# Attention's context product as two column groups of 64 on TensorE, each with the keys of its own two heads

## The chip, the core and the metric

The kernel runs on one core of a Trainium2 chip. The metric is the device time of one execution in microseconds (us): the median of six runs before the change is 1322.69 us, and the six lie between 1321.06 and 1329.03 us. All data are fp32.

A core has four compute engines with queues of their own, each of which works its instructions in order: TensorE (PE in the profile; its weight loads are listed apart as PEld), VectorE (DVE), ScalarE (ACT) and GpSimd (POOL). SyncE (SP) issues most of the DMAs. A matmul has a stationary operand, which a weight load brings into the array, and a moving operand, which streams through it. Its result goes to PSUM, where DVE and ACT read it. Each fp32 matmul of the program appears in the trace as two MATMUL records, each with a weight load; a transpose appears as one.

## The reference

The network has two layers on an input x of 16 samples, 128 channels and 32 x 32 positions. Layer 0 is a linear attention followed by a spectral filter over the tokens, layer 1 is a pair of 3 x 3 convolutions followed by routed experts. Only the attention matters here:

```python
q = jax.nn.softmax(q, axis=-2) * SCALE          # over the 1024 positions
k = jax.nn.softmax(k, axis=-1)                  # over the 32 features of a head
context = jnp.einsum('bhdc,bhec->bhde', k, v)
out = jnp.einsum('bhde,bhdc->bhec', context, q)
y = jnp.einsum('bcn,oc->bon', outf, w_out) + b_out[None, :, None]
```

There are four heads of 32 features. The kernel multiplies in another order: it forms, sample by sample, the 128 x 128 product of q and k over the 1024 positions, of which only the four 32 x 32 blocks on the diagonal (a head's queries with the same head's keys) belong to the result. It sets the rest to zero and multiplies what is left by the output weights, by the value weights and last by the normalised input.

## The kernel before

The program runs in stages: the attention with the tokens' transform (stage A, to about 395 us of the span), the spectral products (to about 685 us), the convolutions with the routing (to about 1216 us), the experts (to about 1290 us) and the output. The change touches stage A only.

Stage A is the class `Attention` (from L341) and an order written out by hand, the list `period` (L713 to L727). One pass of the loop over `p` (L731) issues one step of each kind: the name is a method of `Attention`, the number says for which sample, p + d. So seven samples are under way at once, and a period holds one `tokens`, one `context`, one `channels` and so on, each of another sample. A manual schedule (L730) keeps this order on PE, DVE, ACT and POOL as it is written. The loop starts at p = -6, so the first passes hold only the early steps, and the last passes lack them.

On PE the order in a full period is: `tokens` (8 transposes of the input, L149), `context` (L482), `channels` (8 transposes of the normalised tokens, L159), `input` (8 transposes, L154), `fold` (L495), `even` (L551), `taps_in` (L159), `odd` (L551), `q_tokens` (L149), `fold2` (L504), `k` (L436), `taps` (L618), `group` (L387), `q` (L418) and `out` (L514).

`context` multiplies, for each of the 8 blocks j of 128 positions, the queries of that block (`self.qt[:, j, :]`, stationary, 128 positions by 128 features) by the keys (`ket[:, j, :]`, moving, the same shape), and sums over j in one PSUM tile `pc` of 128 x 128. The keys come from POOL (`k_scale`, L461), the queries from ACT (`q_copy`, L474). `context_mask` (L488, DVE) multiplies `pc` by the reciprocal sums of the queries and by `mask`, which is one on the four 32 x 32 diagonal blocks and zero elsewhere, and writes `cx`. `fold` multiplies `cx` by the output weights, `fold_copy` (L499, DVE) brings the result back, `fold2` multiplies by the value weights, `fold2_copy` (L508, DVE) brings it back, and `out` applies it.

Other steps that the prediction speaks of: `moments` and `moments2` (L132, DVE, four statistics instructions on the transposes in PSUM), `tokens_copy` (L361, ACT), `q_exp` (L427, ACT), `input_copy` (L530, ACT; it follows `moments2`, which reads the same PSUM tile), `channels_copy` (L409, ACT), `out_add` (L519, DVE), `taps_add` (L625, DVE). PSUM is shared out as three large tiles, tag `big`, that go round among eleven steps of a period, and two small ones, tag `s`, which `pc` and the two `pw` take in turn.

Layer 1 holds a step of the form that the change brings in. `pool` (L1242) multiplies, for each of 8 blocks, two stationary operands of 128 x 64 by two moving operands of 128 x 128, into rows 0 to 63 and 64 to 127 of one PSUM tile `pp`:

```python
for i in range(NT):
    for jj in range(2):
        es = slice(jj * E, (jj + 1) * E)
        nc.tensor.matmul(self.pp[es, :], self.gtt[:, i, es], toks[self.b - 1 + jj][:, i, :],
```

Of the kernel before, what the change touches and what calls it, by code (L numbers as in the profile page):

```python
# [8 lines left out]
F32 = mybir.dt.float32  # L9
AF = mybir.ActivationFunctionType  # L10
ALU = mybir.AluOpType
# [3 lines left out]
P = 128  # L15
B, C, H, W = 16, 128, 32, 32
N = H * W
NT = N // 128
# [48 lines left out]
def metaformer_kernel(ctx: ExitStack, tc: tile.TileContext, io: dict, out: bass.AP):  # L67
    nc = tc.nc
# [26 lines left out]
    for n, (g_, b_, m_, v_) in enumerate(((V_G1, V_B1, V_M1, V_V1), (V_G2, V_B2, V_M2, V_V2))):  # L95
# [15 lines left out]
                name=nc.get_next_instruction_name(), ins=[], outs=[], act_func_set_id=EXP_LN  # L111
# [52 lines left out]
    with ExitStack() as l0:  # L164
# [43 lines left out]
        with ExitStack() as a0:  # L208
# [8 lines left out]
            ps = a0.enter_context(tc.tile_pool(name="aps", bufs=2, space=PSUM))  # L217
# [97 lines left out]
            mask = aconst.tile([P, P], F32, name="mask")  # L315
            nc.vector.memset(mask, 0.0)
            for h in range(HEADS):
                s = slice(h * DH, (h + 1) * DH)
# [22 lines left out]
            class Attention:  # L341
# [134 lines left out]
                def context(self):  # L476


                    self.pc = ps.tile([P, P], F32, name="pc", tag="s")
                    ket = self.ke.rearrange("p (j h) d -> p j (h d)", h=HEADS)  # L480
                    for j in range(NT):
                        nc.tensor.matmul(  # L482
                            self.pc, self.qt[:, j, :], ket[:, j, :], start=(j == 0), stop=(j == NT - 1)
                        )

                def context_mask(self):
                    self.cx = work.tile([P, P], F32, name="cx", tag="cx")
                    nc.vector.scalar_tensor_tensor(  # L488
                        self.cx, self.pc, self.qs[:, 2:3], mask, ALU.mult, ALU.mult
                    )  # L490

                def fold(self):
# [253 lines left out]
        with ExitStack() as g0:  # L746
# [61 lines left out]
            for c in range(NCH):  # L808
# [21 lines left out]
                e = cpl.tile([P, JL // RG, 2, C], F32, name="ye", tag="ye", bufs=1)  # L830
# [24 lines left out]
    with ExitStack() as c1:  # L855
# [6 lines left out]
        ps = cps.enter_context(tc.tile_pool(name="cps", bufs=2, space=PSUM))  # L862
# [559 lines left out]
        with tc.manual_schedule(engines=PINNED):  # L1422
            hs, og = {}, {}
# [29 lines left out]
        ps = c1.enter_context(tc.tile_pool(name="fps", bufs=4, space=PSUM))  # L1453
# [147 lines left out]
```

## Time and profile before

| what | value |
|---|---|
| median of six runs | 1322.69 us (1321.06 to 1329.03) |
| the profiled execution's own time | 1324.97 us |
| its span in the trace | 1323.2 us |
| PE busy in the span | 1215.8 us (92%) |
| DVE, ACT, POOL busy | 907.9, 705.1, 502.6 us |
| `context`, L482: matmul records | 256, union 31.2 us |
| mean granted TensorE clock | 0.972 |

The span is the profiled execution from its first to its last instruction; the execution's own time is 1.8 us longer. A row of the timeline holds the start in the span, the time from the first start to the last end, the engine, the line, the operation, the names, the stationary and the moving shape and the number of records; in brackets stands how long the engine was idle before it and whose end released it. A matmul's record lasts longer than its share of the engine, since matmuls are pipelined (275 ns for one of L482): what one costs is the distance from its start to the start of the next. In rows of windows the columns are: the stretch, its length, busy time and records of PE, PEld, DVE, ACT and POOL, the granted clock, the DMA share and GB/s.

### The profile page before, as it was taken

Reading aid. Unit: us, or ns where it says so; the run is one execution under the profiler, and the core shown is the slowest. Engines: PE = TensorE matmul, PEld = TensorE weight load, DVE = VectorE, ACT = ScalarE, POOL = GpSimd, SP = SyncE. Lnnn points to the kernel's source line nnn. Section 1 sums busy time; section 2 is a strip of 40 time slices with the busy share of each in tenths; the row PEclk is TensorE's granted clock in tenths of the full one; section 3 lists DMA queues with packets and bytes.
Section 4 is the critical chain, followed back from the end, with each engine's and each line's share of the span. In section 5 each row is a group of like instructions: output and inputs, shape, how many; then the busy total and the mean of one; then the engine's idle time right before and its main releaser. Section 6 shows DMA issues by size and latency. Waiting matters only on the chain. (4 is left out here: it accounts for less than half of the span.)

```text
span 1323.2 us, 33734 instructions
## 1 busy us (share of the span) xinstructions
PE 1215.8 (92%) x14116; PEld 990.3 (75%) x14116; DVE 907.9 (69%) x1982; ACT 705.1 (53%) x1424; POOL 502.6 (38%) x816
## 2 busy tenths in 40 slices
PE   4889999999998999999956999999999999996885
PEld 3677777777766888888846987989898898883443
DVE  5788788887765666677637777777777686762224
ACT  3777777777545666666623435555555454544111
POOL 2324545454585777777733121222212121110002
PEclk8999999999999999999977999999999999997997
DMA  7014343434344333333266211303122113017986
GB/s 268 17 35 142 116 139 107 146 122 127 117 146 139 129 128 127 129 125 118 98 239 179 69 47 49 93 22 109 32 80 64 33 49 127 17 33 258 374 323 254
DMA packets 87401, 162.99 MB, mean 123 GB/s; under 512 B 5584, under 2 KB 40784, under 8 KB 86864
## 3 DMA queue, kind: packets, MB, share of 16 engines
q1 hardware_dynamic: 86608, 158.33, 36.1%
q8 instruction: 111, 1.82, 0.6%
q0 software_dynamic: 640, 2.49, 0.5%
q14 instruction: 42, 0.34, 0.1%
HBM read 104.18 MB, written 56.62 MB: 122 GB/s over the span
## 5 line engine op out<-in xcount | busy, mean ns | idle before, releaser
L926 PE MATMUL pcv<-v,cw 128*128 128x256 f32 x1536 | 342.9, 380 | 0.0
L926 PEld LDWEIGHTS pcv<-v,cw 128*128 128x128 f32 x1536 | 287.2, 190 | 41.9 <-issue 5.7
L783 DVE COPY g<-pg 128x512 f32<-128x512 f32 x224 | 145.8, 686 | 90.3 <-PE pg L776 90.3
L785 ACT COPY g<-pg 128x512 f32<-128x512 f32 x288 | 153.1, 591 | 101.1 <-PE pg L776 100.9
L776 PE MATMUL pg<-ph,mst 32*128 32x128 f32 x4096 | 153.0, 284 | 4.8 <-ACT g L785 3.4
L776 PEld LDWEIGHTS pg<-ph,mst 32*128 32x128 f32 x4096 | 128.6, 187 | 30.8 <-issue 25.6
L796 PE MATMUL py<-g,v 128*32 128x128 f32 x4096 | 141.0, 278 | 7.6 <-issue 2.3
L796 PEld LDWEIGHTS py<-g,v 128*32 128x32 f32 x4096 | 106.1, 110 | 24.7 <-issue 3.9
L767 POOL TENSOR_TENSOR v<-xc 128x256 f32<-128x256 f32 x128 | 91.5, 740 | 72.1 <-PE py L796 62.8
L141 ACT ACTIVATE tok<-tok,sts 128x128 f32<-128x128 f32 x256 | 101.8, 481 | 23.5 <-POOL sts L1001 20.2
L132 DVE BATCH_NORM_STATS2 bst<-big 128x6 f32<-128x256 f32 x256 | 91.1, 416 | 19.2 <-PE big L154 12.3
L1066 POOL TENSOR_SCALAR sts<-bst 128x8 f32<-128x8 f32 x16 | 6.5, 404 | 234.9 <-DVE bst L132 234.9
L920 DVE TENSOR_TENSOR v<-pads 128x544 f32<-128x544 f32 x128 | 85.0, 723 | 9.8 <-ACT pads L1119 9.5
L618 PE MATMUL big<-u,mu 128*128 128x128 f32 (+4 forms) x384 | 86.0, 380 | 0.0
L274 POOL TENSOR_TENSOR xf<-ab 128x256 f32<-128x256 f32 x34 | 24.8, 729 | 132.8 <-DVE ab L241 132.7
L618 PEld LDWEIGHTS big<-u,mu 128*128 128x128 f32 x384 | 56.8, 191 | 18.0 <-issue 15.3
L1097 ACT ACTIVATE ct<-pcv,bn 128x256 f32<-128x256 f32 x64 | 30.2, 472 | 67.9 <-PE pcv L926 67.0
L551 PE MATMUL big<-wf,ub 128*128 128x256 f32 x256 | 62.0, 385 | 0.2
L149 PEld LDWEIGHTS big<-ident,x 128*128 128x128 f32 x384 | 46.5, 146 | 19.2 <-issue 6.9
L149 PE MATMUL big<-ident,x 128*128 128x128 f32 x384 | 52.8, 283 | 8.7 <-DVE x L1048 3.5
L1115 DVE TENSOR_TENSOR r<-pcv,cs 128x256 f32<-128x256 f32 x64 | 26.9, 420 | 48.6 <-PE pcv L926 47.8
L141 ACT ACTIVATE tt<-tt,sts 128x128 f32<-128x128 f32 x128 | 51.1, 481 | 9.8 <-POOL sts L1001 9.5
(231 smaller groups left out, 2273.1 us busy)
## 6 DMA issues: line engine op xcount, KB each, us to landing
we<-in_weight SPq DMA_DIRECT2D x32, 1024.0 KB, 10.4
vd<-xf SPq DMA_DIRECT2D x16, 1024.0 KB, 5.1
xc<-vd SPq DMA_DIRECT2D x64, 256.0 KB, 3.6
yd<-ys SPq DMA_DIRECT2D x32, 512.0 KB, 3.9
y<-yd SPq DMA_DIRECT2D x15, 896.0 KB, 6.6
x<-in_x SPq DMA_DIRECT2D x16, 512.0 KB, 4.1
mi<-in_M_phi SPq DMA_DIRECT2D x16, 512.0 KB, 4.7
xd<-x SPq DMA_DIRECT2D x16, 512.0 KB, 6.0
```

The costliest lines, as they stand in the source:

```text
L132: nc.vector.bn_stats(bst[:, j : j + 2, :].rearrange("p j s -> p (j s)"), src[:, j : j + 2, :].rearrange("p j c -> p c j"),)
L141: nc.scalar.activation(dst[:, j, :], src[:, j, :], AF.Identity, bias=nm[:, j : j + 1], scale=r[:, j : j + 1],)
L149: nc.tensor.transpose(pt[:, j, :], src[:, j * P : (j + 1) * P], ident)
L551: nc.tensor.matmul(dst, self.ub[:, q, :], wf[:, q, :], start=True, stop=True)
L618: nc.tensor.matmul(self.pa[:, a:hi], mu[:, NF - 1 - si, tap, :], self.u[:, a - tap : hi - tap], start=(tap == 0), stop=(tap == KU - 1),)
L767: nc.gpsimd.tensor_tensor(vv[:, x, 1:, bs], e, o, op)
L776: nc.tensor.matmul(pg[r][:, i], mst[rs, 4 * q + i, :], ph[rs, c, :], start=True, stop=True,)
L783: nc.vector.tensor_copy(dst, src)
L785: nc.scalar.copy(dst, src)
L796: nc.tensor.matmul(py[rows, x, kl, :], v[:, (x * NM + m) * JL + jl, 1 - ri : 3 - ri, :] .rearrange("p k b -> p (k b)"), g[:, ((x * 2 + ri) ...
L920: nc.vector.tensor_tensor(v[:, k], d[i], d[j], op)
L926: nc.tensor.matmul(pc[:, i], wt[:, dy, k, :], v[:, k, hf * HR + dy : hf * HR + dy + HR], start=(dy == 0), stop=(dy == 2),)
```

## The change

Each of the 8 matmuls of a `context` becomes two. Each takes 64 of the queries' features as stationary operand (two heads) and the 64 keys' features of the same two heads as moving operand. The first writes rows 0 to 63 of `pc`, the second rows 64 to 127, both to the same 64 columns, so `pc` is 128 x 64 instead of 128 x 128 and holds for each head its own keys and those of one neighbour. `context_mask` reads `pc` twice over, once for each half of the columns of `cx`, and multiplies by the same mask: the halves that belong to the other two heads become zero as before. Nothing else changes, and no step is moved: PE, DVE, ACT, POOL and SP have the same rows with the same waits in the same order, but for the 128 matmuls of `context` that become 256.

```diff
-                    self.pc = ps.tile([P, P], F32, name="pc", tag="s")
+                    self.pc = ps.tile([P, P // 2], F32, name="pc", tag="s")
                     ket = self.ke.rearrange("p (j h) d -> p j (h d)", h=HEADS)
                     for j in range(NT):
-                        nc.tensor.matmul(
-                            self.pc, self.qt[:, j, :], ket[:, j, :], start=(j == 0), stop=(j == NT - 1)
-                        )
+                        for g in range(2):
+                            hs = slice(g * P // 2, (g + 1) * P // 2)
+                            nc.tensor.matmul(
+                                self.pc[hs, :], self.qt[:, j, hs], ket[:, j, hs],
+                                start=(j == 0), stop=(j == NT - 1), skip_group_check=True,
+                            )
 
                 def context_mask(self):
                     self.cx = work.tile([P, P], F32, name="cx", tag="cx")
                     nc.vector.scalar_tensor_tensor(
-                        self.cx, self.pc, self.qs[:, 2:3], mask, ALU.mult, ALU.mult
+                        self.cx.rearrange("p (g e) -> p g e", g=2),
+                        self.pc.unsqueeze(1).to_broadcast([P, 2, P // 2]), self.qs[:, 2:3],
+                        mask.rearrange("p (g e) -> p g e", g=2), ALU.mult, ALU.mult,
                     )
```

## The prediction

> **What bounds the kernel now.** I read the windows first, cut at the starts of `context`, since the change lies in stage A alone. The second and third columns of a row are the length and PE's busy time:
>
> ```profile
> 54.00:66.00 12.00, 11.05 (x73) 8.53 (x72) 11.65 (x30) 10.48 (x20) 8.14 (x12) 1.00 0.00 0
> 213.40:235.30 21.90, 21.23 (x128) 16.61 (x127) 17.97 (x44) 15.92 (x34) 10.52 (x17) 1.00 0.40 120
> 342.00:357.20 15.20, 15.20 (x89) 12.14 (x88) 11.17 (x24) 9.34 (x19) 7.88 (x12) 1.00 0.47 156
> ```
>
> A full period lasts 21.89 us (`context` starts at 213.43 and 235.32) and PE is idle for 0.66 us of it. The second view is the timeline of that period, to see where PE waits and what stands close behind:
>
> ```profile
> 212.55 1.04 PE L149 MATMUL big<-ident,x 128*128 128x128 f32 x8
> 213.43 1.95 PE L482 MATMUL pc<-ke,qt 128*128 128x128 f32 x16
> 214.05 1.10 ACT L427 ACTIVATE qe<-big,qs 128x1024 f32<-128x1024 f32 x1
> 215.21 1.04 PE L159 MATMUL big<-ident,tok 128*128 128x128 f32 x8
> 215.42 0.35 DVE L488 SCALAR_TENSOR_TENSOR cx<-pc,qs,mask 128x128 f32<-128x128 f32 x1
> 215.46 1.01 ACT L361 COPY tok<-big 128x1024 f32<-128x1024 f32 x1 [0.22 <-PE pc L482]
> 216.09 1.05 PE L154 MATMUL big<-ident,x 128*128 128x128 f32 x8
> 217.18 1.42 DVE L132 BATCH_NORM_STATS2 bst<-big 128x6 f32<-128x256 f32 x4 [0.77 <-PE big L154]
> 217.20 1.89 PE L551 MATMUL big<-wf,ub 128*128 128x256 f32 x8
> 218.69 1.01 ACT L530 COPY ub<-big 128x1024 f32<-128x1024 f32 x1 [2.22 <-DVE bst L132]
> 219.76 1.09 PE L159 MATMUL big<-ident,ub 128*128 128x128 f32 x8 [0.66 <-ACT ub L530]
> ```
>
> The reader is to see that PE's one wait, at 219.76, is the end of a chain that PE itself starts: `input` (L154), `moments2` (L132), `input_copy` (L530). It begins 2.66 us after `context`, so it moves with it. **PE sets the period**, and what `context` takes less is off the period as long as nothing else becomes late. `context` takes 1.79 us (213.43 to 215.21).
>
> **How the new form runs.** The trace has its like: `pool`, with two groups of 64 stationary columns, but 128 moving columns. The third view is the timeline around one, the fourth the records' durations (minimum, median, maximum):
>
> ```profile
> 1188.38 0.60 PE L149 MATMUL big<-ident,x 128*128 128x128 f32 x4
> 1189.97 0.66 PE L149 MATMUL big<-ident,x 128*128 128x128 f32 x4 [0.99 <-DVE x L1145]
> 1190.55 1.97 PE L1242 MATMUL pp<-tt,gtt 128*64 128x128 f32 x32
> 1192.45 1.09 PE L159 MATMUL big<-ident,tt 128*128 128x128 f32 x8
> ```
>
> ```profile
> L1242 PEld LDWEIGHTS pp<-tt,gtt x256: 132/137/231, 843.7 to 1215.7; 128*64 128x64 f32 x128
> L1242 PE MATMUL pp<-tt,gtt x256: 272/273/473, 843.7 to 1215.9; 128*64 128x128 f32 x128
> ```
>
> 32 records take 1.90 us from 1190.55 to 1192.45, where 32 of L482 would take 3.57. The starts of single records show why: they come in pairs 7 ns apart, one of each group, and the pairs 0.109 us apart. So the groups run side by side.
>
> **The sum, term by term.** The distance from a matmul to the next follows the moving columns: four records of L514 (512 columns) take 1.71 us (210.84 to 212.55), 0.428 each; L551 (256) 0.215; transposes (128) 0.109. That is 0.107 for 128 and 0.002 over, hence 0.055 us for 64. Loads follow the stationary columns: when a block starts, sets of loads begin 0.028 us apart for 32 columns (L796, a set of four), 0.055 for 64 (L1242, a set of two), 0.107 for 128 (L776, a set of four). So a pair of 64-column loads, 0.055, has to fit beside a pair of 64-column streams, 0.055. That is the balance that L482 has today at 128 and 128, and there the distance is 0.1115, some 0.004 over the stream alone. I take **0.058 us a pair**; bounds are 0.055 (no such loss) and 0.109 (a pair never goes below `pool`'s).
>
> Changes of form cost something. From the last transpose to `pool`'s first pair it is 0.202 us where an ordinary distance is 0.109; the same stands at L776 to L796 and back, medians 0.200 and 0.202 of some 240. `pool`'s first pair is followed after 0.160 instead of 0.109, since its successor waits for loads that nothing covers. From the last pair to the next step it is 0.210, and that step's second transpose comes after 0.165 instead of 0.110. For the new form the first pair's follower comes after 0.110 (0.160 less the half stream) and the way out takes 0.157 (0.210 less the same).
>
> - Now: 0.109 in, 1.786 for 16 records and the way out, 0.110 to the second transpose of `channels`: 2.005 us.
> - After: 0.202 + 0.110 + 14 x 0.058 + 0.157 + 0.165 = 1.446 us.
> - Difference: **0.56 us a context**; with 0.055 it is 0.60, with everything as in `pool` (1.90 for the block, 0.09 in, 0.05 after) it is a loss of 0.26.
>
> **What of it is on the path.** In the period above these are the waits behind `context` and the distance from their release to their start today: `channels` for `out_add`, 1.17; `input` for `q_exp`'s end with its accumulator read (215.24), 0.85; `fold` for the mask (215.77), 1.21; `even` (L551) for `tokens_copy` (216.47), 0.73; `moments2` for a free DVE (216.41), 0.77. A release takes about 0.06, so the smallest leaves 0.67, and 0.56 fits. What would be late next is `even` on `tokens_copy`, 0.1 us further on; then DVE. The ring that ACT and DVE form by themselves (`input` to `input_copy` to the sums, the norms, `q_exp`, `input`) lasts the period less 0.85, about 21.05 us, so it doesn't bind at 21.33.
>
> `context_mask` keeps its 128 output columns, so I leave its 0.35 us; twice that at worst would lie in DVE's 0.77. Its PSUM operand comes earlier, but it stands behind `moments` (to 215.37) on DVE, so it starts when it did. POOL, SP and all DMAs are untouched.
>
> Not every context counts. The first (54.36) is followed by `fold` at 57.09, 0.06 after the mask on DVE, which is held by other work: nothing. Numbers 2 to 14 count in full: 13 x 0.56 = 7.3. The last two (341.93 and 357.23) have no `channels` behind them; `input` follows, on an x that `out_add` finishes 0.30 before it starts now. Of that 0.06 is the release and 0.05 the uncovered first load, so 0.2 each: 0.4. The later stages start when stage A ends and shift as a whole. **The sum is -7.7 us.** Against the profiled execution's 1324.97 us (span 1323.2) that is 1317.3; this execution is 2.3 us over the median, so I set it against the median: 1322.69 - 7.7 = 1315.0 us, 0.6% less.
>
> **A rule that speaks against it.** In L482 a load begins 3 ns after the matmul before it starts, and the distance is 0.1115 and not the 0.214 that load and stream in turn would take; in `pool` likewise a load starts 2 ns after its group's matmul. The Trainium skill, "TensorE: Matmul & The Clock Gate", section "Part 3: Packing small matmuls — row/col tiling", says that a weight load overlaps running matmuls only where their row groups differ; here both groups use all 128 rows. By that rule pairs would come 0.109 us apart and the change would lose, which is the first rival. The trace doesn't bear the rule out for these forms, so I give it little.
>
> **The rivals.**
>
> - *A pair is no faster than today's matmul* (load 0.055 and stream 0.055 in turn, or the groups one after the other): 0.109 a pair. The sum is then 0.20 to 0.26 us longer a context, over 15 contexts +3.0 to +3.9 us: 1325.7 to 1326.6, slower than before. It decides from a pair distance of 0.095 us on, where 15 distances eat the 0.56. Against it stand the loads 0.055 apart and the overlap in L482; for it, that no row has 64 moving columns. Chance 0.08.
> - *A floor between the two*: the queue must issue 64 instructions in 0.9 us, 14 ns each. The densest stretch known, L796, has four loads and four matmuls in 0.109 us, 13.6 ns each, so there is hardly reserve. A pair at 0.083 gives -2.8: 1319.9. Chance 0.11.
> - *The gain is given back*: `even` or `moments2` becomes late although 0.1 us remain by the rows, say through a slower mask on DVE. If half is lost, -3.9: 1318.8. Chance 0.05.
> - *Forecast*: pair 0.055 to 0.065, -8.4 to -6.2. Chance 0.76.
>
> **How the numbers follow.** The forecast's own range is 1314.3 to 1316.5; the median itself may lie 1 us off on either side, which gives 1313 to 1317.5. To leave out no more than 2 in 10 I reach over the floor's case to 1320; below, to 1312.5, for a smaller price of the change of form. A measurement of this kernel can tell 0.3%, 4.0 us, from no change. Faster by more takes the forecast, half of the third rival and a little of the second: 0.81. Within: the rest of these and most of the first: 0.14. Slower: 0.05.
>
> **What would show it.** In the trace after, a block of 32 records of L484 from `tokens` to `channels` should take 1.08 us instead of 1.79; the pairs should stand 0.058 apart; the distance from the last L149 to the first L484 should be 0.20; a full period should be 21.33 us with PE still idle by about 0.66 before `taps_in` and by nothing before `even`; L491, the mask, should still take 0.35; and the first L776 should start 7.7 us earlier. A distance of 0.11 between pairs, or idle time of PE before L556 of more than a tenth, would make the prediction wrong.

## The result, and the profile after

The changed kernel takes 1316.31 us in the median of 25 runs (1312.50 to 1322.92), beside 1322.96 us for the kernel before in 51 runs: a ratio of 0.9951 with a 95% interval of 0.9938 to 0.9964, or 6.5 us less (4.8 to 8.2). The forecast was 1315.0 us, 7.7 us less. The profiled execution has a span of 1315.7 us. The runs of one kernel spread with the granted clock: of the changed kernel's, those at 0.963 took 1321.7 to 1322.9 us, those at 0.972 took 1312.9 and 1315.8.

The windows first, over one full period from `context` to `context` (length, then PE's busy time and records). It is 21.32 us long where it was 21.89, and PE's idle time in it is the same but for 0.01, 0.68:

```profile
207.71:229.03 21.32, 20.64 (x143) 15.80 (x143) 17.84 (x44) 15.91 (x34) 10.53 (x17) 1.00 0.37 124
```

The timeline of that period, around `context` (L484 now; L154 is `input`, L132 `moments2`, the last row `taps_in`):

```profile
206.74 1.04 PE L149 MATMUL big<-ident,x 128*128 128x128 f32 x8
207.71 1.15 PE L484 MATMUL pc<-ke,qt 128*64 128x64 f32 x32
208.79 1.09 PE L159 MATMUL big<-ident,tok 128*128 128x128 f32 x8
209.47 0.33 DVE L491 SCALAR_TENSOR_TENSOR cx<-pc,qs,mask 128x128 f32<-128x128 f32 x1
209.72 1.04 PE L154 MATMUL big<-ident,x 128*128 128x128 f32 x8
210.79 1.42 DVE L132 BATCH_NORM_STATS2 bst<-big 128x6 f32<-128x256 f32 x4 [0.34 <-PE big L154]
213.37 1.09 PE L159 MATMUL big<-ident,ub 128*128 128x128 f32 x8 [0.66 <-ACT ub L535]
```

The reader is to see three things. From L484 to L159 it is 1.08 us where it was 1.79. The way from L149's start to L484's is 0.97 where it was 0.88: the change of form. And PE's one wait is still 0.66, since its chain moved along, while DVE's idle time before `moments2` fell from 0.77 to 0.34. The mask (L491) takes 0.33 us.

The durations of the records (minimum, median, maximum) show the narrower form:

```profile
L484 PEld LDWEIGHTS pc<-ke,qt x512: 132/138/139, 53.0 to 348.9; 128*64 128x64 f32 x171
L484 PE MATMUL pc<-ke,qt x512: 221/222/271, 53.0 to 348.9; 128*64 128x64 f32 x171
```

By the starts of single records the two groups of a pair stand 6 to 7 ns apart and the pairs 0.0583 us apart.

Two sections of time help to compare traces: the period, and stage A from the first `context` to the first L776 (in after, L781). The latter is 340.83 us before and 332.76 us after, 8.07 less. Behind it and ahead of it the two profiles differ by 0.6 us the other way on balance, in parts of the program that the change doesn't touch. Stage A still holds the distance from the first `context` to the second, which depends on how the kernel started: it lies between 10.67 and 11.95 us in the thirteen traces, and in the changed kernel itself at 11.29 and 11.95. Counted from the second `context` on, stage A is 328.89 us before and 321.47 us after, 7.42 less.

### The profile page after: what moved, and what is told of

It reads as the page before. It is cut to its first block, busy times and chain, and to the rows that moved or that the text cites. A ratio compares the mean times of both kernels' runs of the same rounds, so it can differ in the third digit from the quotient of the medians.

```text
span 1315.7 us, 34246 instructions
## 1 busy us (share of the span) xinstructions
PE 1206.9 (92%) x14372; PEld 977.6 (74%) x14372; DVE 905.1 (69%) x1982; ACT 705.1 (54%) x1424; POOL 502.4 (38%) x816
## 5 line engine op out<-in xcount | busy, mean ns | idle before, releaser
L781 PE MATMUL pg<-ph,mst 32*128 32x128 f32 x4096 | 152.8, 284 | 5.6 <-ACT g L790 4.0
L781 PEld LDWEIGHTS pg<-ph,mst 32*128 32x128 f32 x4096 | 128.5, 187 | 31.7 <-issue 25.2
L132 DVE BATCH_NORM_STATS2 bst<-big 128x6 f32<-128x256 f32 x256 | 91.1, 417 | 15.4 <-PE big L154 8.7
L556 PE MATMUL big<-wf,ub 128*128 128x256 f32 x256 | 62.0, 385 | 0.2
L149 PEld LDWEIGHTS big<-ident,x 128*128 128x128 f32 x384 | 46.6, 146 | 17.8 <-issue 7.2
L149 PE MATMUL big<-ident,x 128*128 128x128 f32 x384 | 52.8, 283 | 7.1 <-ACT tok L141 3.1
```

Source lines behind the costliest of these rows:

```text
L132: nc.vector.bn_stats(bst[:, j : j + 2, :].rearrange("p j s -> p (j s)"), src[:, j : j + 2, :].rearrange("p j c -> p c j"),)
L149: nc.tensor.transpose(pt[:, j, :], src[:, j * P : (j + 1) * P], ident)
L556: nc.tensor.matmul(dst, self.ub[:, q, :], wf[:, q, :], start=True, stop=True)
L781: nc.tensor.matmul(pg[r][:, i], mst[rs, 4 * q + i, :], ph[rs, c, :], start=True, stop=True,)
```

## The experiments

The theory: PE's loop sets the period, pairs of groups run side by side, and a pair's distance follows the moving columns. The rivals: one of the two halves of the change does it alone; the gain comes from elsewhere; the next limit is another than the forecast said.

| run | block of `context`, us | period, us | stage A, us | from the second context, us | median, us | ratio to before (95%) |
|---|---|---|---|---|---|---|
| before | 1.787 | 21.89 | 340.83 | 328.89 | 1322.96 | |
| after | 1.082 | 21.33 | 332.76 | 321.47 | 1316.31 | 0.9951 (0.9938 to 0.9964) |
| e1, after again | 1.083 | 21.33 | 333.49 | 321.54 | 1313.69 | 0.9929 (0.9898 to 0.9960) |
| e2, groups, all keys | 1.898 | 22.15 | 344.25 | 332.98 | 1326.72 | 1.0027 (1.0002 to 1.0051) |
| e3, one group after the other | 1.831 | 22.08 | 343.24 | 331.98 | 1324.85 | 1.0012 (0.9987 to 1.0037) |
| e4, four groups | 0.694 | 21.21 | 330.96 | 319.03 | 1310.50 | 0.9904 (0.9867 to 0.9941) |
| e5, two groups, half the blocks | 0.665 | 21.24 | 330.45 | 319.18 | 1308.22, one run | |
| e6, e4 with `fold` twice | 0.693 | 21.24 | 330.34 | 319.64 | 1318.02 | 0.9954 (0.9925 to 0.9982) |
| e7, after with `fold` twice | 1.082 | 21.33 | 333.23 | 321.97 | 1318.26 | 0.9958 (0.9926 to 0.9990) |
| e8, after with the mask twice | 1.082 | 21.33 | 334.34 | 322.84 | 1320.05, one run | |
| e9, e4 with `q_exp` first | 0.824 | 21.07 | 328.79 | 317.88 | 1311.83 | 0.9928 (0.9903 to 0.9953) |
| e10, e9 with `moments2` first | 0.824 | 21.07 | 329.13 | 318.46 | 1313.86 | 0.9927 (0.9899 to 0.9955) |
| e11, e4 again | 0.694 | 21.21 | 330.96 | 319.03 | 1311.74 | 0.9923 (0.9899 to 0.9948) |

Block and period are read from the full periods of each trace. Each ratio is to runs of the kernel before made beside the run (medians 1322.2 to 1322.7 us), so it isn't quite the quotient of two medians of the table. e5 and e8 have one run each, so only their traces count.

**e1: the changed kernel again.**

> The changed kernel once more, for a narrower interval and as the neighbour of the others. Theory (PE sets the period, each context is 0.56 us shorter): ratio to the kernel before 0.994 to 0.995, block of L484 1.08 us, period 21.33 us. Rival (the 6.7 us are partly the start of the kernel, whose first context began 1.3 us earlier in the profile of after): ratio 0.996 to 0.998 while the period is the same 21.33.

Period and block are the same to 0.01 us, and the ratio is 0.9929; the rival's 0.996 is the end of the interval. Of the 8.07 us in the profile of after, 0.65 were the start, since the first two contexts stand 11.29 us apart there and 11.95 in e1; counted from the second context the two traces save 7.42 and 7.35. The gain isn't an accident of one start.

**e2: the grouping without the halved stream.** `pc` is 128 x 128 again, with the old mask:

```diff
-                                self.pc[hs, :], self.qt[:, j, hs], ket[:, j, hs],
+                                self.pc[hs, :], self.qt[:, j, hs], ket[:, j, :],
```

> Two column groups of 64, but each with all 128 moving columns, and the mask as before: the grouping without the halved stream. Theory (pair distance follows the stream): pairs 0.109 us apart as in pool, block 1.90 us, 0.09 more on the way in and 0.05 behind, period 22.15 us, about 3.9 us slower than the kernel before. Rival (two groups side by side are what brings the gain, the halved keys are not needed): block near 1.1 us, as fast as after.

```profile
213.15 1.97 PE L484 MATMUL pc<-ke,qt 128*64 128x128 f32 x32
215.05 1.09 PE L159 MATMUL big<-ident,tok 128*128 128x128 f32 x8
```

The block takes 1.90 us, as `pool`'s does, and the pairs are 0.109 apart. The kernel is slower than before: +4.1 us from the second context on (+3.4 in the whole of stage A, whose first distance was short in this start, 11.28 us), ratio 1.0027. Two groups alone only cost the change of form; the gain is in the halved keys.

**e3: the halved stream without neighbours.**

```diff
-                    for j in range(NT):
-                        for g in range(2):
+                    for g in range(2):
+                        for j in range(NT):
```

> The changed kernel with the two loops exchanged: the 8 blocks of the first group, then the 8 of the second, the same 16 program matmuls with 64 moving columns. Theory (the groups must run side by side): single matmuls 0.058 us apart, 32 of them, block about 1.97 us, period about 22.25 us, some 5 us slower than before. Rival (the halved stream alone brings the gain, since neighbours overlap anyway): block near 1.1 us, as fast as after.

```profile
212.86 1.90 PE L484 MATMUL pc<-ke,qt 128*64 128x64 f32 x32
214.69 1.09 PE L159 MATMUL big<-ident,tok 128*128 128x128 f32 x8
```

Single records are 0.0583 us apart, so one alone costs what a pair costs. The gain is gone: +3.1 us from the second context on, and the ratio's interval holds 1. The block is 0.14 shorter than I expected: around the change from the first group to the second the starts come in three pairs 3 to 6 ns apart, as if the last records of one group ran beside the first of the other. So both parts of the change are needed, the halved keys and the two groups in turn.

**e4: four groups of 32.** `pc` is 128 x 32 and needs no other head's keys at all:

```diff
-                        for g in range(2):
-                            hs = slice(g * P // 2, (g + 1) * P // 2)
+                        for g in range(HEADS):
+                            hs = slice(g * DH, (g + 1) * DH)
```

> Four column groups of 32, each with its own head's 32 keys; pc is 128 x 32 and read four times over by the mask. Theory 1 (distance is the stream plus 0.004, no other floor): sets of four 0.031 us apart, block about 0.64 us, context 1.0 us shorter than in the kernel before; of that only 0.67 us a period can count, because then even waits for tokens_copy: period 21.22 us, 1.4 us faster than after, PE idle 0.3 us before even. Theory 2 (instructions cannot be issued closer than the 13.6 ns each of the densest stretch known): sets of four 0.109 us apart, block about 1.85 us, period about 22.05 us, some 2 to 3 us slower than the kernel before.

```profile
206.51 0.76 PE L484 MATMUL pc<-ke,qt 128*32 128x32 f32 x64
207.21 1.09 PE L159 MATMUL big<-ident,tok 128*128 128x128 f32 x8
208.04 0.19 ACT L427 ACTIVATION_READ_ACCUMULATOR qe<-big,qs 128x1 f32 x1
208.29 1.16 PE L154 MATMUL big<-ident,x 128*128 128x128 f32 x8
208.45 1.01 ACT L361 COPY tok<-big 128x1024 f32<-128x1024 f32 x1 [0.22 <-DVE bst L132]
209.52 1.99 PE L556 MATMUL big<-wf,ub 128*128 128x256 f32 x8
212.06 1.09 PE L159 MATMUL big<-ident,ub 128*128 128x128 f32 x8 [0.55 <-ACT ub L535]
```

Sets of four are 0.032 us apart at first and 0.036 on average in the second half, so 128 instructions go out in 0.69 us, some 5 ns each: there is no floor at 14 ns. With 0.20 in and 0.165 behind, the context is 0.94 us shorter than before, but the period only 0.68, to 21.21. That is the number that I had expected, for the reason that `even` waits for `tokens_copy`. The rows show a second wait: `input` (L154) starts 0.06 after `q_exp`'s accumulator read ends (208.23) and has 1.16 us of records instead of 1.04. The 0.3 us of idle time before `even` (L556) that I had expected aren't there, since `input` is late already; but `even` does start 0.06 after `tokens_copy` ends (209.46), and has 1.99 us of records instead of 1.89. Which of the two sets the period is what e5 to e7 and e9 ask.

**e5: half the blocks.** Only every second block of positions is summed, so half of the sum is left out:

```diff
-                    for j in range(NT):
+                    for j in range(0, NT, 2):
```

> The changed kernel (two groups) with only every second of the 8 blocks: half of the sum over the positions is left out. Block of L484 about 0.61 us, so PE alone would need a period of 20.86 us. Theory (below a saving of about 0.7 us a period something else than PE's work sets it, as with the four groups): period 21.2 us as there, with PE waiting before input for q_exp. Rival (the four groups lost 0.26 us a period to their own irregular issue): period 20.9 us.

With two groups and a context that would allow 20.86, the period is 21.24. The block takes 0.665 us, 0.05 more than expected, for which the list of waits names no cause. The limit isn't peculiar to four groups. Over eight periods PE waits in `input` for ACT as the expectation says (us in total, times, longest); the changed kernel has no such wait:

```profile
PEld big L154 <- ACT qe L427: 2.5, 8, 0.3
```

**e6 and e7: `fold` twice**, in the kernel with four groups and in the changed one:

```diff
-                    nc.tensor.matmul(self.pw, self.cx, wout, start=True, stop=True)
+                    for _ in range(2):
+                        nc.tensor.matmul(self.pw, self.cx, wout, start=True, stop=True)
```

> Four groups, and fold's matmul issued twice (0.22 us more of PE between input and even). Theory A (with four groups the ring of ACT and DVE sets the period through q_exp and input, and PE's wait before taps_in covers what lies between input and taps_in): period stays 21.21 us, PE's idle time before taps_in falls from 0.55 to about 0.35. Theory B, the step of the prediction (even is late, on tokens_copy, and sets the period): even starts 0.2 us later than with the four groups alone, period 21.35 to 21.42 us, 2 us slower than the four groups.

> The changed kernel, and fold's matmul issued twice (0.22 us more of PE between input and taps_in). Theory A (PE's loop runs over tokens, context, channels, input and then over DVE and ACT to taps_in; what PE does between input and taps_in is covered by the 0.66 us of idle time): period stays 21.33 us, idle before taps_in 0.44. Theory B (every PE instruction of a period counts, as the prediction put it: PE sets the period): period 21.55 us, 2.9 us slower than after.

The timeline of e6, then that of e7; the first row is `fold`, the second `even`, the third `taps_in`:

```profile
210.51 0.61 PE L501 MATMUL pw<-wout,cx 128*128 128x128 f32 x4
210.96 1.89 PE L557 MATMUL big<-wf,ub 128*128 128x256 f32 x8
213.29 0.87 PE L159 MATMUL big<-ident,ub 128*128 128x128 f32 x6 [0.44 <-ACT ub L536]
```

```profile
210.52 0.61 PE L501 MATMUL pw<-wout,cx 128*128 128x128 f32 x4
210.97 1.89 PE L557 MATMUL big<-wf,ub 128*128 128x256 f32 x8
213.31 0.88 PE L159 MATMUL big<-ident,ub 128*128 128x128 f32 x6 [0.44 <-ACT ub L536]
```

In both `even` starts 0.2 us later and the wait before `taps_in` is shorter, 0.44 instead of 0.55 and 0.66. The periods are 21.24, 0.03 over e4's, and 21.33: they don't follow. Work between `input` and `taps_in` is free up to that wait, and a late `even` is too. Theory B falls for both. In e6 the wait fell by less than the 0.2 us expected, since `even` starts too late there to be held by `tokens_copy`, and its records take 1.89 us again. From the second context on, stage A is 0.4 to 0.6 us longer than in e1 and e4; 0.15 to 0.18 of that lies behind each of the last two contexts. The medians of these two lie 2 to 8 us above those of their neighbours, with intervals that overlap. In the profiled executions that difference lies behind stage A, in stages that these edits don't touch: 933.6 us in e6 beside 925.6 in e4, and 931.3 in e7 beside 924.9 in e1. In e6 the clock is granted at half for 73.9 us of that time, in e4 for 58.4; by my estimate the 15.5 us between them are worth 7.8, if PE is busy in all of them. In e7 and e1 it is 59.4 and 56.7 us, which doesn't account for the 6.4; that stays open.

**e8: the mask twice on DVE**, with `for _ in range(2):` before the operation of `context_mask`.

> The changed kernel with context_mask issued twice on DVE, 0.37 us more between moments and moments2. DVE is idle for 0.34 us before moments2 in after, so moments2 starts about 0.03 us late and, lying on the loop, lengthens the period by as much: 21.36 to 21.38 us. Rival (the mask has a follower that waits, fold on PE): fold starts late, but that is covered before taps_in, so nothing more than the 0.03; if the mask were on the path the period would be 21.7 us.

The period stays 21.33 us, without the 0.03 to 0.05 expected. The two operations take 0.72 us, and `moments2` starts 3.09 us behind the start of `context`, as in after: the idle time before it took up the second mask, as the prediction had it. The longer stage A doesn't come from the periods: from the second context to the third it is 16.71 us beside 15.40 in after, and there the clock is granted at half for 6.8 us instead of 3.4.

**e9 and e10: lift the limit.** In the list `period`, over the kernel with four groups, first `q_exp` and `k_exp` change places, then also `moments2` and `group_scale` (the edit of e10, its two lines drawn into one):

```diff
-("group_root", 4), ("k_exp", 3), ("fold", 2), ("group_scale", 4), ("moments2", 1), ("q_exp", 3),
+("group_root", 4), ("q_exp", 3), ("fold", 2), ("moments2", 1), ("group_scale", 4), ("k_exp", 3),
```

> Four groups, and on ACT q_exp issued before k_exp instead of after it. Theory A (with four groups input waits for q_exp): the wait goes, input comes 0.26 us earlier, of which DVE's 0.22 us of idle time before moments2 lets nearly all pass: period 20.95 to 21.0 us, 3 us faster than the four groups alone (about 1307). Theory B (even on tokens_copy sets the period with four groups): tokens_copy stays where it is behind moments, period unchanged at 21.21.

> As the run before, and on DVE moments2 issued before the four small operations of group_scale instead of behind them, so that DVE is free 0.7 us earlier for moments2. Theory A: nothing holds input and moments2 back, PE's loop alone is left: period 20.95 us, 3.1 us faster than the four groups. If group_scale now comes late for channels_copy, the wait stands before channels_copy and odd, and the period is 21.1 or more.

The period falls to 21.07, half of the way to 20.95: theory B, in which nothing moves, is out, and `q_exp` was the limit. The size was off because the wait moved. In e9's waits of eight periods `input` no longer appears, and `channels` waits instead, which leaves its block at 0.82:

```profile
PEld big L159 <- ACT qe L427: 1.4, 8, 0.2
```

The missing part is that wait: the block is 0.13 longer than in e4. e10 changes nothing more, where 20.95 was expected: DVE is idle for 0.7 us before `moments2` and the period is the same, so DVE doesn't hold it.

**e11: four groups again.**

> The four groups again beside these two, for a fair comparison: period 21.21 us, ratio to the kernel before about 0.993 by the trace's stage A (9.9 us), between that and 0.990 as first measured.

Period 21.21, stage A 330.96 as in e4, ratio 0.9923. Counted from the second context on, four groups are 2.4 to 2.5 us shorter than the changed kernel, and they are faster than both kernels by their medians; against the changed kernel the intervals of the ratios overlap. The swap of e9 takes another 1.2 us off behind the second context (the rest of the 2.2 in stage A is the start), which the medians can't tell.

## Why the prediction was right

- **PE's loop sets the period: right, with a correction.** 0.56 us off `context` takes 0.56 off a full period (21.89 to 21.33), and e2's 0.26 more puts 0.26 on. But not all of PE counts. e7 shows that the loop runs from `input` over DVE and ACT to `taps_in`, and that PE's own work on that stretch lies beside it.
- **The price of a pair: right.** 0.058 taken, 0.0583 measured. The loads run beside the streams: a group's next load starts 2 to 3 ns after its matmul. The first rival, by which load and stream take turns, would have given 0.109. The rule of the Trainium skill behind it ("TensorE: Matmul & The Clock Gate", section "Part 3: Packing small matmuls — row/col tiling": a weight load overlaps running matmuls only where row groups differ) doesn't hold here: both groups use all rows, and the measured distance decides.
- **The change of form: right.** 0.202 in, 0.100 + 0.007 to the second pair, 0.159 out and 0.166 to the second transpose were forecast as 0.202, 0.110, 0.157 and 0.165.
- **The floor of issue: the rival is out**; e4 issues at some 5 ns an instruction.
- **Which contexts count: right but for the second and the last two.** The second gives 0.38, not 0.56 (15.78 to 15.40 to the third). Behind it PE waits 2.88 us for `fold_copy` in both kernels, and the clock is then granted at half for 3.41 us. In before (the first two rows; 0.50 is the granted clock) PE still waited in the first 0.35 of that, in e1 (the last row) it was busy in all of it:

```profile
73.64:73.99 0.35, 0.00 (x0) 0.00 (x0) 0.35 (x4) 0.32 (x3) 0.00 (x0) 0.50 0.00 0
73.99:77.05 3.06, 3.06 (x14) 3.06 (x15) 2.79 (x14) 3.03 (x9) 0.00 (x0) 0.50 0.00 0
72.80:76.21 3.41, 3.41 (x18) 3.41 (x18) 3.13 (x16) 3.38 (x9) 0.27 (x1) 0.50 0.00 0
```

  So from `fold2` to `group` it is 3.74 us in e1 and 3.56 before. The 0.18 between them, half of the 0.35, is what is missing: where the stretch fell, and not what `context` takes. e2, where PE was busy in all of it too, is 0.43 over before here, 0.17 more than the 0.26 of its period. The next twelve give 0.56 each. The last two give 0.28 together, not 0.4 (15.30 to 15.18, and 37.96 to 37.80 from the last to the first L776). There `input` waits for `out_add`, as foreseen:

```profile
332.82 1.15 PE L484 MATMUL pc<-ke,qt 128*64 128x64 f32 x32
334.27 1.16 PE L154 MATMUL big<-ident,x 128*128 128x128 f32 x8 [0.30 <-DVE x L524]
```

  The loads of L154 are 0.19 long, those of L159 0.14, and its second matmul after a wait comes after 0.21 and not 0.165. The prediction had carried over the wrong row.
- **The first context counts for nothing: right.** To the second it is 11.94 us before and 11.95 in e1, where `fold` waits for the mask:

```profile
56.19 0.49 PE L500 MATMUL pw<-wout,cx 128*128 128x128 f32 x2 [0.46 <-DVE cx L491]
```

  In the profile of after it is 11.29, but also 11.28 in e2, whose context is the longest. That distance depends on how the start of the kernel went, not on the context: after, e2, e3, e5 and e7 (11.26 to 11.29) have 3.4 us at half the clock between 48 and 52 us, just ahead of the first context, and before, e1, e4 and e11 (11.93 to 11.95) have none there. How the one leads to the other no run shows.
- **What would be late next: wrong.** The step said `even` on `tokens_copy`, at 0.67 us a period. In e4 `even` does wait for it, but a late `even` is covered by the wait before `taps_in` (e6, e7). The limit is `input` on `q_exp`: 0.85, less 0.06 for the release and 0.12 because the first loads after a wait are uncovered (1.16 us of records for 1.04). That makes 0.67 too, so e4's period came out as expected for the wrong reason, and only e6 and e9 told the two apart.
- **The sum.** By its parts it is 0.4 + 12 x 0.56 + 0.3 = 7.4, and the two traces give 7.42 and 7.35 from the second context on, beside the forecast's 7.7. The 0.3 too much are the second context and the last two. The median's 6.5 (4.8 to 8.2) holds both; the rest of 0.9 us is within the spread of the runs and not explained further.

## What to carry to other kernels

A matmul of which half or less of the output is used can be cut into column groups if the moving operand is cut along with the stationary one; cutting one alone gains nothing here. The price is the change of form, here some 0.09 us in, 0.05 at the second pair and 0.1 out with the uncovered loads, so a block must be long enough to pay it. Slack has to be taken along the loop that sets the period: a step that comes late is no limit where a longer wait of the same engine behind it takes the lateness up, as `even` showed, and a number that comes out right doesn't show that its reason was.

## What the runs showed of the hardware

- With 64 or fewer moving columns the distance still follows the columns and the loads: 0.0583 us for 64 and 0.032 to 0.036 for 32, where 128 take 0.109 to 0.112.
- PE issued four loads and four matmuls in 0.032 us (e4), more than three times as densely as in the densest stretch of the kernel before (L796, eight in 0.109); after some 32 matmuls the regular sets of four give way to starts 15 and 2 ns apart in turn, at 0.033 us for four.
- Matmuls of one column group, issued one after the other, were 0.0583 us apart, and only around the change of group did three pairs run side by side (e3).
- Behind PE's wait of 2.5 to 2.9 us before the second `fold2` the clock was granted at half for 3.41 us in before, after and e1, and for 6.8 in e8. It wasn't in e11, whose wait of 2.54 us is as long as that of e4, the same kernel, which had it.
